# Score rows through DRAM and VectorE's 32x32 transposes in place of TensorE's, in a fused four-layer graph attention kernel

## The chip, the core and the metric

The kernel runs on one core of a Trainium2 chip. Its engines are TensorE (PE, matmuls; its weight loads are listed as PEld), VectorE (DVE), ScalarE (ACT), GpSimd (POOL) and SyncE (SP, which here only issues DMA transfers). Each engine works through its own list of instructions in order and waits at semaphores for the others. The metric is the device time of one execution in microseconds (us).

## The reference: four graph attention layers

There are 128 graphs of 128 nodes, each with 512 float32 features (`x`) and a 128x128 0/1 adjacency matrix (`adj`, int32, symmetric, ones on the diagonal). Four layers follow each other, each of the form `x = x + layer(relu(layernorm(x)), adj)`:

```python
# layer 0: e = leaky_relu(h@W.T@a1 + (h@W.T@a2).T); softmax over columns where adj != 0
x = x + elu(softmax(masked e) @ h)
# layer 1: two attention stages; the first with 4 heads of 256, elu, then one head of 512
xl = (h @ W1).reshape(N, 4, 256); e[s, d, head] = leaky_relu(asrc[s] + adst[d])
h = elu(attention over s, per head, + b1); x = x + attention(h @ W2) + b2
# layer 2: scores from two vectors of 512, the diagonal always allowed
x = x + softmax(masked leaky_relu(src[:, None] + dst[None, :] + b)) @ h
# layer 3: 8 heads of 64
xh = (h @ W_proj) per head; x = x + relu(softmax(masked leaky_relu(a_src[i] + a_dst[j] + b)) @ xh)
```

In every attention a score is a sum of a number that belongs to its row and one that belongs to its column. So a 128x128 tile of scores needs one of the two vectors as a column (one number per partition, which is how the engines produce it) and the other as a row repeated over all 128 partitions.

## The kernel before

The four layers are fused: a graph's `x` tile (128 nodes on partitions, 512 features) is loaded once, goes through all layers in SBUF and is stored. One graph is one generator, `graph(b)`, that yields single instructions. A planner written in the kernel (`Scheduler`) keeps `FLYING = 11` graphs under way and puts their instructions in one order. It estimates when each could start from a table of costs (`Step.estimate`) and gives an engine, among the steps that could start about then, the one with the lowest rank. A rank is the graph's age times the pace of the busiest engine, plus a due time spread over `FLYING` paces, from a rehearsal of one graph. Buffers come from tagged pools of fixed size (`tile_of(tag, bufs, ...)`): a stream that asks for one when none has been returned stands still. As every step is recorded by one line of the planner, nearly all instructions carry line 301 in the profile and are told apart by their tiles' names.

How a column becomes a row over all partitions:

- **By TensorE.** `attended` (layer 0, layer 1's second attention, layer 2) multiplies the column, broadcast to 128x128, with the identity (`T.transpose(pb[:, :P], other.to_broadcast([P, P]), ident)`, line 707): the rows stand in a PSUM bank. In the trace these are `bank<-ident,f` (layers 0 and 2) and `bank<-ident,x` (layer 1).
- **By DRAM.** `rows_in_dram` (608) has VectorE transpose 32x32 squares (`r<-...`, STREAM_TRANSPOSE), then SP writes four short pieces to DRAM (`d<-r`) and a second transfer reads them back, repeated for all partitions. Layer 1's first attention (`e<-d`) and layer 3 work so.
- The last `LATE = 5` graphs use TensorE throughout (`spread`, `add_rows`).

Layer 1's first attention ends with a turn of the four heads' weights: `turned` (588) lets VectorE transpose all 32x32 squares in place, and exchanges the squares by four writes to DRAM and one load (`turned<-e`, `et<-turned`).

Layer 3 (`layer3`, 860) builds its eight heads' scores already turned, which saves that turn. ScalarE first copies the turned mask `m3t` over eight heads into `e` (`e<-m3t`). The row vectors and, later, the negated maxima come through DRAM, and GpSimd adds each to `e` by a DMA that accumulates in SBUF (`added`, 649, `e<-d` on POOL's queue). The maxima need the scores in the other direction too, so SP loads the other vector into `d3` (`d<-d`), and VectorE sums it with the mask `m3` and takes the maxima. Then come eight Prelu, the second accumulating DMA and one Exp over all 1024 columns.

The turned mask comes from TensorE: `graph` (983) transposes `m3` (`bank<-ident,m`), VectorE makes the mask of layer 1 out of it (`m1<-bank,off_diag`), and ScalarE copies it to `m3t`. `load` (967) brings four graphs' `adj` at a time by one transfer (`at`).

Of the kernel before, what the change touches and what calls it, by code (L numbers as in the profile page):

```python
# [21 lines left out]
FLYING = 11  # L22
PATIENCE = .3
LANES = 8
AHEAD = 1
LATE = 5
# [18 lines left out]
class Step:  # L45
# [19 lines left out]
    def estimate(self, name, outs, ins, kw):  # L65

        if name == "dma_start":
            moved = size(outs[0]) * outs[0].shape[0] * 4
            if self.engine == "POOL":
                self.moves = moved / 165e3  # L70
                return 1.0, 3
            run = 4 * min(a.shape[-1] for a in outs + ins)
            self.moves = moved / (280e3 if run > 512 else 220e3)
            busy = 0.5 if max(len(a.shape) for a in outs + ins) > 2 else 0.35
            return busy, (2.2 if moved > 16384 else 0.6)
# [250 lines left out]
def kernel(  # L326
# [62 lines left out]
    off_diag = const.tile([P, P], F32, name="off_diag")  # L389
    nc.vector.tensor_scalar(off_diag, ident, -1.0, 1.0, ALU.mult, ALU.add)  # L390
# [36 lines left out]
    def setup():  # L427
# [7 lines left out]
        for c in range(KC):  # L435
            if c % 2 == 0:
                pair = yield tile_of("e3", 3, H3, P)
                pair = pair.rearrange("p h q -> p (h q)").rearrange("p (c f) -> p c f", c=2)
            w0.append(pair[:, c % 2])
            yield S.dma_start(out=w0[c], in_=l0_w[c * P : (c + 1) * P])  # L440
# [4 lines left out]
        yield Fork(fold_w1())  # L445
        yield from load(1)
# [19 lines left out]
        wa = yield tile_of("e3", 3, H3, P)  # L466
        wa = wa.rearrange("p h q -> p (h q)")[:, : H3 * 2 * K3]
# [120 lines left out]
    def turned(t, squares, tag, bufs):  # L588

        yield V.transpose(squares, squares)
        f = t.shape[1] // R
        d = dram.tile([R, Q, R, f], F32, tag="turned", name="turned")
        yield Group(
            [
                S.dma_start(
                    out=d[:, :, r].rearrange("m b f -> b m f"),
                    in_=t[r * Q : (r + 1) * Q].rearrange("b (m f) -> b m f", m=R),
                )  # L600
                for r in range(R)
            ]
        )
        to = yield tile_of(tag, bufs, R * f)
        yield S.dma_start(out=to, in_=d.rearrange("m b r f -> (m b) (r f)"))
        return to
# [16 lines left out]

    def repeated(cols):
        n = cols.shape[1]
        return cols.unsqueeze(1).to_broadcast([P, Q // n, n])
# [13 lines left out]

    def add_rows(cols, to):

        for g in range(0, cols.shape[1], 4):
            pt = yield from spread(cols[:, g : g + 4])
            part = to[:, g * P : (g + 4) * P]
            yield V.tensor_tensor(part, pt, part, ALU.add)
            give_back(pt)

    def added(to, rows):

        yield G.dma_start(out=to, in_=rows, accum_op=ALU.add)
# [51 lines left out]
    def attended(own, other, mask, values, exact=False):  # L703

        e = yield tile_of("e0", 3, P)
        pb = yield bank()
        yield T.transpose(pb[:, :P], other.to_broadcast([P, P]), ident)
        c, rz = yield from attention(own, [pb[:, :P]], [e], mask, exact)
# [45 lines left out]
    def layer0(xt, mask):  # L754
# [6 lines left out]
        pa, c, rz = yield from attended(f[:, 0:1], f[:, 1:2], mask, h, exact=True)  # L761
# [10 lines left out]
    def layer1(xt, mask, late):  # L772
# [28 lines left out]
        else:  # L801
            to = yield from turned(e, e, "et1", 2)
# [40 lines left out]
        pa, c, rz = yield from attended(gx[:, 1:2], gx[:, 0:1], mask, gx[:, E2:])  # L843
# [4 lines left out]
    def layer2(xt, mask):  # L848
# [6 lines left out]
        pa, c, rz = yield from attended(fb, f[:, 1:2], mask, h)  # L855
# [4 lines left out]
    def layer3(xt, mask, mask_t, late):  # L860

# [8 lines left out]

        e = yield tile_of("e3", 3, H3, P)
        yield A.copy(e, mask_t.unsqueeze(1).to_broadcast([P, H3, P]))
        give_back(mask_t)
# [11 lines left out]
        yield G.tensor_tensor(f, fx[:, :, :E3].rearrange("p h s -> p s h"), b_l3, ALU.add)  # L885
        if late:
            fork = yield Fork(add_rows(f[:, 1], e.rearrange("p h q -> p (h q)")))
        else:
            rows = yield from rows_in_dram(repeated(f.rearrange("p s h -> p (s h)")), 2 * H3)
            d = yield tile_of("d3", 2, H3, P)  # L890
            yield S.dma_start(out=d.rearrange("p h q -> p (h q)"), in_=rows[:, : H3 * P])
            fork = yield Fork(added(e.rearrange("p h q -> p (h q)"), rows[:, H3 * P :]))

        for g in range(0, H3, 4):
            if late:
                d = yield from spread(f[:, 0, g : g + 4])
                part = d.rearrange("p (h q) -> p h q", h=4)
            else:
                part = d[:, g : g + 4]
# [3 lines left out]
                        out=part[:, j],  # L903
                        in0=part[:, j],
                        in1=mask,
# [9 lines left out]
            if late:  # L915
                give_back(d)
        give_back(mask)
        if not late:
            give_back(d)
        yield Join(fork)  # L920
# [3 lines left out]
        fork = None if late else (yield Fork(rows_in_dram(repeated(mx), H3)))  # L924
        for k in range(H3):
            yield A.activation(
                out=e[:, k, :],
                in_=e[:, k, :],
                func=AF.Prelu,
                bias=f[:, 0, k : k + 1],  # L930
                alpha=SLOPE,
            )
        ef = e.rearrange("p h q -> p (h q)")
        fork = yield Fork(add_rows(mx, ef) if late else added(ef, (yield Join(fork))))
        yield Join(fork)
        yield A.activation(out=ef, in_=ef, func=AF.Exp)
        t = yield tile_of("t", 5, D)
        for i in range(2):
# [6 lines left out]
                        lhsT=e[:, k, :],  # L945
# [16 lines left out]
        give_back(e, fx, f)  # L962
        yield V.scalar_tensor_tensor(xt, t, 0.0, xt, ALU.max, ALU.add)
# [3 lines left out]
    def load(b):  # L967
# [3 lines left out]
        if b % AG == 0:  # L971
# [3 lines left out]
            )  # L975
        sched.reached.add(("x", b))

    def not_above_0(a):
        m3 = yield tile_of("m3", 4, P)
        yield V.tensor_scalar(m3, a, 0.0, NEG, ALU.is_le, ALU.mult)  # L980
        return m3

    def graph(b):
        if FLYING + AHEAD <= b + AHEAD < B:
            yield Fork(load(b + AHEAD))
        yield Until(("x", b))
# [3 lines left out]
        yield from layer0(xt, m0)  # L990
        give_back(m0)
        m3 = yield from not_above_0(a)
        m3t = yield tile_of("m3t", FLYING, P)
        m1 = yield tile_of("m1", 8, P)
        pt = yield bank()
        yield T.transpose(pt[:, :P], m3, ident)
        give_back(m3)
        yield V.tensor_tensor(m1, pt[:, :P], off_diag, ALU.mult)
        yield A.copy(m3t, pt[:, :P])
        give_back(pt)  # L1000
        yield from layer1(xt, m1, b >= B - LATE)
# [4 lines left out]
        yield from layer2(xt, m2)  # L1006
        give_back(m2)
        m3 = yield from not_above_0(a)
        yield from layer3(xt, m3, m3t, b >= B - LATE)
        yield S.dma_start(out=out[b], in_=xt)  # L1010

    adjs, xs = {}, {}
    with tc.manual_schedule():
        sched.rehearse(load(0))
        sched.plan(sched.rehearse(graph(0)))
# [59 lines left out]
```

## Time and profile before

| | |
|---|---|
| median of 3 runs | 3332.38 us (3332.28 to 3333.03) |
| the profiled execution's own time | 3333.2 us |
| its span in the profile | 3331.4 us |
| TensorE busy | 3286.5 us, 16252 matmul records |
| weight loads busy | 2577.7 us |
| VectorE busy | 2752.8 us, 11063 instructions |
| ScalarE busy | 2478.1 us |
| GpSimd busy | 1208.4 us, of it 246 DMA issues at 948 ns |
| DMA | 380.90 MB, mean 114 GB/s; SP's queue 248.06 MB, GpSimd's 128.99 MB |

The profile is one execution. "Busy" is the time in which at least one instruction of the engine was under way. The slices cut the span into 40 equal parts, and a digit is the busy share in tenths. In the groups a line reads: source line, engine, operation, output tile from input tiles, shapes, count, then busy time, mean ns of one, and the idle time of the engine just before such instructions with what ended it. A table of stretches gives, for each, the busy time of every engine with its number of instructions, then the clock that TensorE was granted, the DMA engines' busy share and the GB/s they moved. An order of time lists start, duration, engine, operation and count. Program order on an engine is fixed, so an instruction that waits holds up all behind it.

### The profile page before, as it was taken

Reading aid. Unit: us, or ns where it says so; the run is one execution under the profiler, and the core shown is the slowest. Engines: PE = TensorE matmul, PEld = TensorE weight load, DVE = VectorE, ACT = ScalarE, POOL = GpSimd, SP = SyncE. Lnnn points to the kernel's source line nnn. Section 1 sums busy time; section 2 is a strip of 40 time slices with the busy share of each in tenths; the row PEclk is TensorE's granted clock in tenths of the full one; section 3 lists DMA queues with packets and bytes.
Section 4 is the critical chain, followed back from the end, with each engine's and each line's share of the span. In section 5 each row is a group of like instructions: output and inputs, shape, how many; then the busy total and the mean of one; then the engine's idle time right before and its main releaser. Section 6 shows DMA issues by size and latency. Waiting matters only on the chain. (4 is left out here: it accounts for less than half of the span.)

```text
span 3331.4 us, 59808 instructions
## 1 busy us (share of the span) xinstructions
PE 3286.5 (99%) x16252; PEld 2577.7 (77%) x16252; DVE 2752.8 (83%) x11063; ACT 2478.1 (74%) x6932; POOL 1208.4 (36%) x2559
## 2 busy tenths in 40 slices
PE   7999999999999999999999999999999999999997
PEld 5777777777777777777777777777777777777776
DVE  5878888888888888888888888888888888888866
ACT  4677777777777777777777777777777777777764
POOL 1233343343343343333334334334334334334321
PEclk7999999999999999999999999999999999999998
DMA  5144444454445454454545454445445545545430
GB/s 156 50 111 116 118 122 115 121 121 119 113 123 121 116 124 119 114 125 114 120 121 120 116 118 121 121 115 123 118 115 124 121 115 120 121 114 123 93 85 29
DMA packets 253730, 380.90 MB, mean 114 GB/s; under 512 B 59088, under 2 KB 138448, under 8 KB 253392
## 3 DMA queue, kind: packets, MB, share of 16 engines
q1 hardware_dynamic: 213792, 248.06, 25.7%
q0 software_dynamic: 35424, 128.99, 20.8%
q8 instruction: 130, 2.13, 0.3%
q14 instruction: 208, 1.70, 0.2%
q10 hardware_dynamic: 4176, 0.02, 0.1%
HBM read 309.35 MB, written 67.57 MB: 113 GB/s over the span
## 5 line engine op out<-in xcount | busy, mean ns | idle before, releaser
L301 PE MATMUL bank<-w2x,y 128*128 128x257 f32 x4096 | 972.1, 380 | 0.0
L301 PE MATMUL bank<-w1x,ht 128*128 128x344 f32 x3072 | 957.4, 455 | 0.7 <-ACT ht L301 0.7
L301 PEld LDWEIGHTS bank<-w2x,y 128*128 128x128 f32 x4096 | 759.4, 190 | 218.5 <-issue 119.6
L301 PEld LDWEIGHTS bank<-w1x,ht 128*128 128x128 f32 x3072 | 567.7, 191 | 243.3 <-issue 7.8
L301 ACT ACTIVATE h<-xt,st 128x512 f32<-128x512 f32 x512 | 416.5, 814 | 257.4 <-POOL st L301 256.2
L301 POOL TENSOR_SCALAR st<-st 128x1 f32<-128x1 f32 x1024 | 351.4, 347 | 661.8 <-DVE st L301 539.5
L301 ACT ACTIVATE e<-e,c 128x128 f32<-128x128 f32 x1408 | 532.7, 400 | 77.8 <-DVE e L301 59.0
L301 PE MATMUL bank<-wpx,ht 128*128 128x264 f32 x2048 | 501.9, 389 | 1.7 <-ACT ht L301 1.7
L301 PEld LDWEIGHTS bank<-wpx,ht 128*128 128x128 f32 x2048 | 390.5, 191 | 66.5 <-ACT ht L301 2.4
L301 ACT ACTIVATE e<-e,f 128x128 f32<-128x128 f32 x1152 | 386.1, 392 | 2.6 <-POOL st L301 1.5
L301 POOL DMA_DIRECT2D e<-d x246 | 233.3, 948 | 389.1 <-DMA d<-r 208.7
L301 DVE BATCH_NORM_STATS2 st<-xt 128x6 f32<-128x512 f32 x512 | 349.4, 683 | 0.0
L301 PEld LDWEIGHTS bank<-x,e 128*128 128x128 f32 x2048 | 269.4, 193 | 91.4 <-issue 56.7
L301 POOL TENSOR_TENSOR st<-st,minus_half 128x1 f32<-128x1 f32 x512 | 298.5, 585 | 29.4
L301 PE MATMUL bank<-et,xl 128*128 128x128 f32 x2048 | 270.3, 275 | 0.0
L301 PE MATMUL bank<-x,e 128*128 128x65 f32 x2048 | 259.0, 270 | 8.9 <-ACT e L301 8.9
L301 POOL TENSOR_TENSOR f<-f 128x8 f32<-128x8 f32 x128 | 30.7, 240 | 651.3 <-DVE f L301 449.1
L301 PE MATMUL bank<-h,et 128*128 128x512 f32 x512 | 263.8, 597 | 1.8 <-ACT et L301 1.8
L301 PEld LDWEIGHTS bank<-et,xl 128*128 128x128 f32 x2048 | 254.0, 192 | 4.9 <-issue 0.5
L301 DVE TENSOR_TENSOR y<-bank,b 128x512 f32<-128x512 f32 x256 | 176.1, 688 | 97.3 <-PE bank L301 95.8
L301 DVE CUSTOM_DVE_ANT_0 d<-d,m 128x128 f32<-128x128 f32 x984 | 225.3, 284 | 34.9 <-DMA d<-d 33.8
L301 POOL TENSOR_SCALAR m<-m 128x128 f32<-128x128 f32 x128 | 143.3, 1119 | 288.9 <-DVE m L301 266.1
(86 smaller groups left out, 5334.4 us busy)
## 6 DMA issues: line engine op xcount, KB each, us to landing
e<-d POOLq DMA_DIRECT2D x246, 512.0 KB, 7.1
d<-d SPq DMA_DIRECT2D x123, 512.0 KB
xt<-in_x_dram SPq DMA_DIRECT2D x128, 256.0 KB
e<-d SPq DMA_DIRECT2D x128, 256.0 KB
out_dram<-xt SPq DMA_DIRECT2D x128, 256.0 KB
turned<-e SPq DMA_DIRECT2D x492, 64.0 KB
et<-turned SPq DMA_DIRECT2D x123, 256.0 KB
at<-in_adj_dram SPq DMA_DIRECT2D x32, 256.0 KB
```

The costliest lines, as they stand in the source:

```text
L301: method(*args, **kw)
```

## The change

- **Rows.** A new `row(col)` takes TensorE's place in `attended`: VectorE transposes the column's squares, SP writes four pieces of 32 numbers to DRAM (`d<-r`) and reads them back over all partitions (`row<-d`, 64 KB). TensorE's way stays for the last 5 graphs, and in layer 0 for the first `EARLY = 8` graphs.
- **Layer 3** now makes its scores unturned: SP loads the row vectors straight into `e`, VectorE adds the mask and takes the maxima in place, and ScalarE does eight Prelu and eight Exp with a bias by column. Then `exchanged` (once `turned`, now without VectorE's transpose in it) sends the squares through DRAM into `et3`, and VectorE transposes them from there into `e`. The mask copy over eight heads, `d3`, both accumulating DMAs and the second row vector are gone. The last 5 graphs turn their scores by TensorE (`bank<-ident,e`).
- **The turned mask.** `load_turned` loads `adj` a second time, four graphs at once by four transfers, with the 32x32 squares already exchanged (runs of 128 bytes); one VectorE transpose of 128x512 for four graphs turns the squares. `m1` comes from it in one instruction; TensorE's transpose, `m3t` and one `m3` go.
- **The planner.** `FLYING` goes from 11 to 13 (which also sizes the pools of `x`, `adj` and DRAM tiles), small DMAs are costed at 1.3 instead of 0.6 us, runs of at most 128 bytes at a lower rate, and the rehearsed graph is graph 8. `e3` and `w0`'s use of it change shape only; `m3` has 3 buffers instead of 4.

```diff
-FLYING = 11
+FLYING = 13
+EARLY = 8
...
-            self.moves = moved / (280e3 if run > 512 else 220e3)
+            self.moves = moved / (280e3 if run > 512 else 220e3 if run > 128 else 130e3)
...
-            return busy, (2.2 if moved > 16384 else 0.6)
+            return busy, (2.2 if moved > 16384 else 1.3)
...
+        yield Fork(load_turned(0))
         yield from load(1)
...
-    def turned(t, squares, tag, bufs):
-        yield V.transpose(squares, squares)
+    def exchanged(t, tag, bufs):
...
+    def row(col):
+        r = yield tile_of("r", 5, Q)
+        yield V.transpose(r, col.to_broadcast([P, Q]))
+        d = dram.tile([R, Q], F32, tag="d1", name="d")
+        yield S.dma_start(out=d, in_=r[::Q])
+        give_back(r)
+        to = yield tile_of("row", 3, P)
+        yield S.dma_start(out=to, in_=d.rearrange("c b -> (c b)").partition_broadcast(P))
+        return to
...
-    def attended(own, other, mask, values, exact=False):
+    def attended(own, other, mask, values, late, exact=False):
         e = yield tile_of("e0", 3, P)
-        pb = yield bank()
-        yield T.transpose(pb[:, :P], other.to_broadcast([P, P]), ident)
-        c, rz = yield from attention(own, [pb[:, :P]], [e], mask, exact)
+        if late:
+            rows = yield bank()
+            yield T.transpose(rows[:, :P], other.to_broadcast([P, P]), ident)
+        else:
+            rows = yield from row(other)
+        c, rz = yield from attention(own, [rows[:, :P]], [e], mask, exact)
...
-        e = yield tile_of("e3", 3, H3, P)
-        yield A.copy(e, mask_t.unsqueeze(1).to_broadcast([P, H3, P]))
...
+        e = yield tile_of("e3", 3, H3 * P)
         if late:
-            fork = yield Fork(add_rows(f[:, 1], e.rearrange("p h q -> p (h q)")))
+            heads = e.rearrange("p (h c b) -> p h c b", h=H3, b=Q)
         else:
-            rows = yield from rows_in_dram(repeated(f.rearrange("p s h -> p (s h)")), 2 * H3)
-            d = yield tile_of("d3", 2, H3, P)
-            yield S.dma_start(out=d.rearrange("p h q -> p (h q)"), in_=rows[:, : H3 * P])
-            fork = yield Fork(added(e.rearrange("p h q -> p (h q)"), rows[:, H3 * P :]))
+            heads = e.rearrange("p (c h b) -> p h c b", h=H3, b=Q)
+            rows = yield from rows_in_dram(repeated(f[:, 0]), H3, True)
+            yield S.dma_start(out=e, in_=rows)
...
-        fork = None if late else (yield Fork(rows_in_dram(repeated(mx), H3)))
-        for k in range(H3):
-            yield A.activation(
-                out=e[:, k, :],
-                in_=e[:, k, :],
-                func=AF.Prelu,
-                bias=f[:, 0, k : k + 1],
-                alpha=SLOPE,
-            )
-        ef = e.rearrange("p h q -> p (h q)")
-        fork = yield Fork(add_rows(mx, ef) if late else added(ef, (yield Join(fork))))
-        yield Join(fork)
-        yield A.activation(out=ef, in_=ef, func=AF.Exp)
+        for bias, func in ((f[:, 1], dict(func=AF.Prelu, alpha=SLOPE)), (mx, dict(func=AF.Exp))):
+            for k in range(H3):
+                yield A.activation(
+                    out=heads[:, k], in_=heads[:, k], bias=bias[:, k : k + 1], **func
+                )
+        et = []
+        if late:
+            for g in range(0, H3, 4):
+                et += yield from transposed(blocks_of(e)[g : g + 4], "ht", 3)
+        else:
+            to = yield from exchanged(e, "et3", 2)
+            yield V.transpose(
+                e.rearrange("p (h r b) -> p r h b", h=H3, b=Q),
+                to.rearrange("p (r h b) -> p r h b", h=H3, b=Q),
+            )
...
+    def load_turned(b):
+        adjs_t[b // AG] = t = adjp.tile([P, AG, P], I32, tag="at_t", name="at_t")
+        yield Group(
+            [
+                S.dma_start(
+                    out=t[m * Q : (m + 1) * Q].rearrange("b g (r c) -> b (g r) c", r=R),
+                    in_=adj[b : b + AG, :, m * Q : (m + 1) * Q].rearrange(
+                        "g (r b) c -> b (g r) c", r=R
+                    ),
+                )
+                for m in range(R)
+            ]
+        )
...
-        m3 = yield from not_above_0(a)
-        m3t = yield tile_of("m3t", FLYING, P)
-        pt = yield bank()
-        yield T.transpose(pt[:, :P], m3, ident)
-        yield V.tensor_tensor(m1, pt[:, :P], off_diag, ALU.mult)
-        yield A.copy(m3t, pt[:, :P])
+        if b % AG == 0:
+            yield Until(("loaded", b // AG))
+            flat = adjs_t[b // AG].rearrange("p g j -> p (g j)")
+            yield V.transpose(flat, flat)
+            sched.reached.add(("turned", b // AG))
+        yield Until(("turned", b // AG))
+        at = adjs_t[b // AG][:, b % AG, :]
+        m1 = yield tile_of("m1", 8, P)
+        yield V.scalar_tensor_tensor(m1, at, 0.0, neg_off_diag, ALU.is_le, ALU.mult)
```

## The prediction

> **What bounds the kernel now.** I read the busy shares and the 40 slices first, then busy time by stretch, then the order of time on TensorE, then the costliest groups.
>
> ```profile
> PE 3286.5 (99%) x16252; PEld 2577.7 (77%) x16252; DVE 2752.8 (83%) x11063; ACT 2478.1 (74%) x6932; POOL 1208.4 (36%) x2559
> ...
> PE   7999999999999999999999999999999999999997
> ...
> DVE  5878888888888888888888888888888888888866
> ...
> PEclk7999999999999999999999999999999999999998
> ```
>
> TensorE (PE) is full except in the first and last slice. Those are also where its granted clock falls. The stretches:
>
> ```profile
> 30.00:40.00 10.00, 8.23 (x36) 7.03 (x36) 5.57 (x26) 3.45 (x9) 1.48 (x3) 0.50 1.10 290
> ...
> 90.00:100.00 10.00, 8.45 (x47) 6.79 (x46) 9.47 (x26) 8.27 (x24) 1.09 (x3) 1.00 0.09 27
> 100.00:110.00 10.00, 10.00 (x51) 8.14 (x50) 9.47 (x29) 4.50 (x13) 1.21 (x3) 1.00 0.26 79
> ...
> 400.00:2800.00 2400.00, 2400.00 (x11939) 1888.22 (x11938) 2025.89 (x8213) 1837.97 (x5161) 916.54 (x1907) 1.00 0.49 119
> ```
>
> The columns are PE, weight load, VectorE (DVE), ScalarE (ACT), GpSimd (POOL), clock, DMA share, GB/s. From 400 to 2800 us PE is busy 2400.00 of 2400 us at full clock. A usual graph has 125 matmul records (32 with w2x, 24 with w1x, 16 each with wpx, et and x, 6 of attention, 15 transposes), so 11939 records are 95.5 graphs and the pace is 25.1 us a graph. In it DVE is busy 2025.89 / 95.5 = 21.2 us and ACT 19.2 us.
>
> Busy is not the same as full, since matmul records overlap. The starts decide:
>
> ```profile
> 1610.14 1.00 PE L301 MATMUL bank<-x,e 128*128 128x65 f32 x8
> 1610.98 0.28 PE L301 MATMUL bank<-ident,m 128*128 128x128 f32 x1
> 1611.09 0.27 PE L301 MATMUL bank<-ident,e 128*128 128x128 f32 x1
> 1611.20 1.90 PE L301 MATMUL bank<-w2x,y 128*128 128x257 f32 x8
> 1612.93 0.39 PE L301 MATMUL bank<-wpx,ht 128*128 128x264 f32 x1
> ```
>
> A transpose lasts 0.27 us, but the next matmul starts 0.11 us after it. Eight matmuls with w2x take 1612.93 - 1611.20 = 1.73 us, 0.216 each. Over the 2400 us the mean distance from one start to the next is that of its kind's median (ident,f 109 ns, ident,m 116, w2x 217, w1x 289), so no gap is left and each matmul taken away saves its distance. The Trainium skill (Perfetto Trace Analysis, Identifying the Most-Contended Engine) says matmul busy time is a poor measure of how near TensorE is to its limit, and that weight-load busy time is a better one. That row is 77%, so by the rule a quarter of PE might be free, removed transposes might be worth nothing, and the sum would stay at 3333. The start distances decide against that here.
>
> ```profile
> L301 PE MATMUL bank<-ident,f 128*128 128x128 f32 x376 | 86.3, 275 | 4.8 <-POOL f L301 2.8 <-DVE f L301 2.0
> ...
> L301 DVE STREAM_TRANSPOSE e<-e 128x512 f32<-128x512 f32 x123 | 85.3, 693 | 2.0 <-ACT e L301 1.8
> ...
> L301 DVE STREAM_TRANSPOSE r<-f 128x32 f32<-128x32 f32 x246 | 50.8, 207 | 34.8 <-POOL f L301 26.4
> ```
>
> The first is one of the three kinds of PE transpose that go; the others price what comes. Then who waited for whom (total, times, longest), on the engines and in SP's own DMA queue, for layer 3's score rows as they are today:
>
> ```profile
> DVE d L301 <- DMA d<-d: 33.8, 44, 2.0
> ```
>
> ```profile
> SPq L301 <- DMA d<-r: 508.9, 339, 5.1
> ```
>
> **The change part by part, TensorE.** Counted in the two programs: transposes of score columns (ident,f) fall from 376 to 58, of x from 128 to 5, of the mask (ident,m) from 128 to 0; transposes of e rise from 404 to 444 (the last five graphs' layer 3 now turns its scores at the end). Net 318 + 123 + 128 - 40 = 529 fewer, by 0.11 us: **-58.2 us**. Nothing else on PE changes. A usual graph goes from 25.1 to 24.7 us.
>
> **VectorE**, per graph. Added: three column transposes of 128x32 (3 x 0.207 = 0.62), one layer 3 transpose of 128x1024 (twice the 0.693 row, 1.39), a quarter of adj's 128x512 (0.17). Gone: one 128x32 (0.21), one of two not_above_0 masks (0.22). The mask m1, the score sums and their maxima change operands, not count; the row for 128x128 sums is 284 ns from SBUF and 287 from PSUM. Net +1.75, so 23.0 of 24.7 us: 93%, where it had 84%. The large transpose writes in strides that no row shows. Bounds: 1.39 (a row of half its size, and the 128x32 rows read in strides without cost) and double that, 2.77, which would make 24.4 of 24.7. I take 1.39, the row of the same operation. Either way it lies beside PE.
>
> **ScalarE**, per graph: gone are the copy of the mask over eight heads (1.03), m3t (0.27) and the Exp over 1024 (1.05); added are eight Exp of 128. One such takes 0.39 in its row, but the last graph's chain of eight takes 2.35 us in the trace, 0.29 each. Net 0, at most +0.8 by the 0.39: 81% of 24.7. Hidden.
>
> **GpSimd** loses 246 adding transfers at 0.948 us of issue, 233 us in all, and the 7.1 us each took to land.
>
> **SP and DMA.** SP issues more: per usual graph 3 row writes, 3 row loads, one for adj_t (four per four graphs), and in layer 3 five exchange transfers, with four writes fewer there and the score load kept. Eight more at 0.34 to 0.45 us are some 3 us, on about 8. Behind a row write its load waits at SP (508.9 / 339 = 1.5 us a time), and other graphs' loads and the output are queued behind that: three such waits more a graph and one more for layer 3's exchange, 6 us. 8 + 3 + 6 and today's waits of 508.9 / 123 = 4 stay under 24.7, with less to spare than now. In bytes the 129 MB of adding transfers are traded for 129 MB of exchange at a DMA share of 0.49, so bandwidth is free in the middle. Of small transfers the change adds 722 (361 of 0.5 KB and 361 of 64 KB). The skill (DMA: Bandwidth & Descriptors, Rules for kernel authors) speaks against such transfers: under 64 KB one pays mostly overhead, and its section on one DMA's anatomy gives about 2 us of fixed cost each. By that page a row's two hops would be an estimated 4 us late, 12 us more in a graph's life, and the sum would not move as long as other graphs cover it; no run here shows a row of this kind yet.
>
> **Latency.** A row through DRAM costs two hops at about 1.5 us plus issue, transpose and queue; I call it 5, thrice 15 us a graph. In layer 3 two landings of 7.1 go, and an exchange comes (write to read about 6 us in the same trace for layer 1, then the landing): +10. Net some +11 us in a graph's life, against 13 x 24.7 - 11 x 25.1 = 45 us more that 13 graphs in flight allow. Cover: the other twelve graphs.
>
> **Ramp and tail.** In the first 40 us DMA runs at a share of 0.88 to 1.10 and the clock at half, so new traffic there delays PE: four second adj loads of 256 KB, one more first load and two more x are 1.75 MB, at 290 GB/s 6 us if all comes before the weights, 0 if none does. I take 4. First graphs keep their layer 0 rows on PE; the x transposes begin only at 113 us. In the tail the last layer 3 trades an addition (0.70) and a 1.05 Exp for eight short ones (2.35) and a transpose with copy: +1. More graphs in flight may fill the tail better or put off its last graph: -10 to +10.
>
> **Sum** against the profiled execution (3333.2, span 3331.4): 3333.2 - 58.2 + 4 + 1 = 3280.0. It lies 0.8 above the median of 3332.38, so 3279 for a median.
>
> **Rivals.** (1) *PE keeps its pace only nearly.* The cushion of ready work in front of PE shrinks as DVE goes to 93%. At 95% DVE, 90 to 100 us shows PE at 8.45 and 100 to 110 at 10.00, so both happen. PE at 99% instead of 100% for the middle 3100 us costs 31: 3310; from 0.4% to 1.5%: 3291 to 3326.
> (2) *VectorE becomes the bound because its queue waits for landings.* Each of the three row sums and the layer 3 transpose stands in DVE's order, and everything behind it waits when its DMA is late. DVE has 24.7 - 23.0 = 1.7 us a graph free: waits over 0.43 us each make it the bound, over 0.53 each end above today's pace. At 0.77 (33.8 / 44, what a late score load costs today when it waits) it is 26.1 a graph, +1.0 over today for 123 graphs: 3455. At 0.6: 25.4, 3370. Against it: today's same wait falls on 44 of 123 loads, 0.27 us as a mean, below 0.43.
> (3) *The transposes were free*, so that the 0.11 us stays as a gap: 3333 to 3338. Against it: the start distances.
>
> **How the numbers follow.** PE stays full: 0.62 (own range 3265 to 3291: ramp 0 to 6, tail -10 to +10). Rival 1: 0.17. Rival 2: 0.13. Rival 3 or gain and losses cancelling: 0.05. Below 3265, a ramp or tail that shrinks: 0.03. Executions agree within 0.03%; 0.2% (7 us) is about what can be told from no change: faster 0.82, same 0.05, slower 0.13. The range 3260 to 3332 leaves out rival 2 (0.13), the cancelling case's upper half and the gains below 3260, some 0.17.
>
> **What would show it.** Right: PE 100% from 400 to 2800 us with about 97 graphs there, ident,f x58, no ident,m, DVE 90 to 94% and no large idle before the sums on row. Wrong: idle before e<-row put down to DMA d or row, PE nines with idle released by DVE or ACT, the layer 3 transpose well over 1.39 us, or a lower clock after 200 us.

## The result and the profile after

The changed kernel takes 3290.93 us (median of 4 runs, 3290.09 to 3293.56) against 3332.33 us before (4 runs, 3330.88 to 3333.03). The ratio is 0.9881, 95% interval 0.9869 to 0.9894. The forecast was 3279, range 3260 to 3332: the direction and the range held, the value was 12 us too low. The profiled execution after took 3290.5 us, with a span of 3288.7.

The busy shares of the page after, and TensorE's, VectorE's and the clock's row of the 40 slices:

```profile
PE 3233.0 (98%) x15723; PEld 2529.1 (77%) x15723; DVE 2839.9 (86%) x11308; ACT 2546.5 (77%) x7582; POOL 911.3 (28%) x2313
...
PE   6999999999999999999999999999999999999997
...
DVE  6778888988888988888898988898888888888875
...
PEclk6999999999999999999999999999999999999998
```

529 matmul records are gone (16252 to 15723), and TensorE is full but for the ends, as before. The stretches after (PE, weight load, VectorE, ScalarE, GpSimd, clock, DMA share, GB/s):

```profile
30.00:40.00 10.00, 8.80 (x35) 7.23 (x35) 4.63 (x18) 3.67 (x9) 0.00 (x0) 0.50 1.11 312
40.00:50.00 10.00, 0.48 (x3) 0.39 (x2) 9.59 (x28) 0.22 (x2) 0.00 (x0) 0.50 0.91 163
50.00:60.00 10.00, 3.47 (x5) 1.05 (x5) 8.19 (x27) 4.62 (x10) 3.13 (x9) 0.50 0.00 0
60.00:70.00 10.00, 5.05 (x7) 1.64 (x7) 8.70 (x30) 3.50 (x8) 0.78 (x2) 0.50 0.00 1
...
400.00:2800.00 2400.00, 2399.02 (x11720) 1882.38 (x11719) 2137.87 (x8550) 1913.93 (x5713) 688.29 (x1741) 1.00 0.46 131
```

and the stretch of before beside the second of them:

```profile
40.00:50.00 10.00, 10.00 (x32) 6.42 (x33) 7.12 (x22) 4.71 (x11) 0.00 (x0) 0.79 0.16 55
```

The middle is nearly as forecast (PE busy 2399.02 of 2400 us). The start is not: between 40 and 70 us TensorE works 9 of 30 us, at half clock. The groups after that answer to those shown of before, and the two new ones:

```profile
L302 DVE CUSTOM_DVE_ANT_0 e<-row,m 128x128 f32<-128x128 f32 x361 | 101.7, 282 | 51.3 <-DMA row<-d 50.7
...
L302 DVE STREAM_TRANSPOSE e<-et 128x1024 f32<-128x1024 f32 x123 | 148.6, 1208 | 0.2 <-issue 0.2
...
L302 DVE STREAM_TRANSPOSE e<-e 128x512 f32<-128x512 f32 x123 | 86.6, 704 | 4.9 <-ACT e L302 4.9
```

```profile
L302 PE MATMUL bank<-ident,f 128*128 128x128 f32 x58 | 11.3, 288 | 5.0 <-DVE f L302 4.8 <-POOL f L302 0.2
```

The waits after, of VectorE for the new rows and of SP's queue for the row writes:

```profile
DVE e L302 <- DMA row<-d: 50.7, 60, 3.0
```

```profile
SPq L302 <- DMA d<-r: 393.1, 450, 4.5
```

**A yardstick for all runs.** In the middle of the kernel before no gap is left between matmuls. So I give every matmul record the mean distance to the next start that its kind has there (400 to 2800 us), and call the sum of these over a whole run its *work*: the time TensorE needs if it never waits and its clock is full. Kinds that do not occur there (112 records of the setup, and 80 of the last graphs after the change) count by their shape, or at 0.11 us. The span less the work is the *loss*, so it holds waits, late starts and slow clock together.

| us | before | after | difference |
|---|---|---|---|
| span | 3331.4 | 3288.7 | -42.7 |
| work | 3250.1 | 3191.5 | -58.6 |
| loss, first 400 us | 44.9 | 59.5 | +14.6 |
| loss, 400 us to 200 before the end | 0.6 | 9.0 | +8.4 |
| loss, last 200 us | 35.8 | 28.8 | -7.0 |

The work fell by what was forecast (58.2), and the middle stays within 9.0 us of it. What was missed lies in the loss, +14.6 of it at the start.

### The profile page after: what moved, and what is told of

Same layout as the page of the kernel before. It is cut to its first block, busy times and chain, and to the rows that moved or that the text cites. A ratio compares the mean times of both kernels' runs of the same rounds, so it can differ in the third digit from the quotient of the medians.

```text
span 3288.7 us, 60292 instructions
## 1 busy us (share of the span) xinstructions
PE 3233.0 (98%) x15723; PEld 2529.1 (77%) x15723; DVE 2839.9 (86%) x11308; ACT 2546.5 (77%) x7582; POOL 911.3 (28%) x2313
## 4 chain that ended last, share of the span: by engine, by line
PE 95%; DVE 2%; DMA 2%; ACT 1%; SPq 0%; issue 0%; POOL 0%; ACTq 0%; DVEq 0%; POOLq 0%
PE bank L302 95%; DVE e L302 0%; SPq L302 0%; ACT e L302 0%; DMA d<-r 0%; DVE products L302 0%; DVE t L302 0%; POOL st L302 0%; DMA row<-d 0%; DMA w1x<-in_L_gnn_W_dram 0%; ACT h L302 0%; DMA xt<-in_x_dram 0%; DVE xt L302 0%; DVE st L302 0%; DMA at<-in_adj_dram 0%
## 5 line engine op out<-in xcount | busy, mean ns | idle before, releaser
L302 PE MATMUL bank<-w2x,y 128*128 128x257 f32 x4096 | 959.1, 381 | 0.0
L302 ACT ACTIVATE e<-e,f 128x128 f32<-128x128 f32 x2176 | 739.4, 392 | 18.2 <-DVE c L302 18.0
L302 ACT ACTIVATE e<-e,c 128x128 f32<-128x128 f32 x1408 | 543.5, 396 | 78.7 <-DVE c L302 59.7
L302 DVE CUSTOM_DVE_ANT_0 e<-e,m 128x128 f32<-128x128 f32 x1496 | 344.0, 284 | 4.2 <-DMA e<-d 3.0
L302 POOL TENSOR_TENSOR st<-st,minus_half 128x1 f32<-128x1 f32 x512 | 313.2, 612 | 40.6 <-POOL st L302 0.2
L302 ACT COPY xl<-bank 128x344 f32<-128x344 f32 x384 | 169.5, 442 | 188.9 <-PE bank L302 187.6
L302 PEld LDWEIGHTS bank<-x,e 128*128 128x128 f32 x1968 | 248.5, 192 | 19.7 <-issue 8.6
L302 POOL TENSOR_SCALAR m<-m 128x128 f32<-128x128 f32 x128 | 86.3, 674 | 619.3 <-DVE m L302 503.8
L302 DVE SCALAR_TENSOR_TENSOR xt<-bank,c,xt 128x512 f32<-128x512 f32 x256 | 192.0, 750 | 75.5 <-PE bank L302 70.3
L302 PE MATMUL bank<-x,e 128*128 128x65 f32 x1968 | 246.7, 268 | 0.0
```

What stands on the lines that cost most here:

```text
L302: method(*args, **kw)
```

## The experiments

All are edits of the changed kernel unless said otherwise. In the table "rows" are the score rows of layers 0, 1 (second attention) and 2, "mask" the turned mask (TensorE's transpose, or adj's second load), "n" the graphs in flight; loss is given for the three stretches of the table above. The ratio is to runs of the kernel before that belong to the same set (medians 3331.51 for e1 to e4, 3330.69 for e5 to e8, 3331.05 for e9 to e12). Work and loss come from one profiled execution each, which need not be the median one: it lies 4.8 us under the median for e4, 3.1 under it for e3, 2.5 under it for e1, and 5.1, 4.2 and 2.9 over it for e10, e7 and e11. So a difference of some us between losses is not yet a difference between kernels.

| kernel | rows | layer 3 | mask | n | median us | ratio (95%) | work | loss: start, middle, end |
|---|---|---|---|---|---|---|---|---|
| before | TensorE | old | TensorE | 11 | 3332.33 | 1 | 3250.1 | 44.9, 0.6, 35.8 |
| after | DRAM | new | 2nd load | 13 | 3290.93 | 0.9881 (0.9869 to 0.9894) | 3191.5 | 59.5, 9.0, 28.8 |
| e1 | DRAM | new | 2nd load, early | 13 | 3289.70 | 0.9874 (0.9858 to 0.9891) | 3191.5 | 55.6, 9.1, 29.1 |
| e2 | DRAM | new | 2nd load | 11 | 3359.09 | 1.0080 (1.0065 to 1.0095) | 3191.5 | 77.9, 46.3, 41.6 |
| e3 | TensorE | new | 2nd load | 13 | 3484.83 | 1.0457 (1.0441 to 1.0472) | 3230.9 | 67.5, 158.0, 23.5 |
| e4 | DRAM | new | TensorE | 13 | 3301.66 | 0.9906 (0.9891 to 0.9921) | 3206.4 | 47.2, 14.8, 26.7 |
| e5 | TensorE | old | TensorE | 13 | 3342.23 | 1.0033 (1.0021 to 1.0045) | 3250.1 | 51.7, 10.7, 28.0 |
| e6 | TensorE | new | 2nd load | 11 | 3377.20 | 1.0139 (1.0122 to 1.0156) | 3230.9 | 58.2, 58.7, 28.5 |
| e7 | DRAM | old | 2nd load | 13 | 3428.69 | 1.0293 (1.0274 to 1.0313) | 3195.8 | 72.7, 127.0, 35.5 |
| e8 | DRAM | new | as e1, one fold on GpSimd | 13 | 3291.18 | 0.9882 (0.9867 to 0.9897) | 3191.5 | 58.0, 9.4, 28.5 |
| e9 | DRAM, all | new | 2nd load | 13 | 3291.10 | 0.9879 (0.9864 to 0.9894) | 3190.6 | 56.2, 14.8, 28.5 |
| e10 | TensorE | old | 2nd load | 13 | 3370.38 | 1.0118 (1.0103 to 1.0133) | 3235.2 | 57.5, 51.5, 29.3 |
| e11 | TensorE | new | TensorE | 11 | 3321.54 | 0.9970 (0.9958 to 0.9981) | 3245.8 | 43.5, 5.3, 28.1 |
| e12 | DRAM | new | as e1, other order | 13 | 3288.41 | 0.9872 (0.9857 to 0.9886) | 3191.5 | 58.4, 11.4, 25.3 |

### The start: where the 15 us went

The order of time of the changed kernel, from SP's issue of adj's second loads to the first matmuls of layer 1 (start, duration; idle time before in brackets):

```profile
38.01 10.82 SPq L302 DMA_DIRECT2D at_t<-in_adj_dram  x16
...
49.51 0.28 DVE L302 TENSOR_SCALAR e<-e,f 128x128 f32<-128x128 f32 x1
...
50.70 0.48 PE L302 MATMUL bank<-ident,e 128*128 128x128 f32 x1 [10.22 <-ACT e L302]
...
67.09 0.70 DVE L302 STREAM_TRANSPOSE at_t<-at_t 128x512 int32<-128x512 int32 x1
67.83 0.29 DVE L302 SCALAR_TENSOR_TENSOR m<-at_t,neg_off_diag 128x128 f32<-128x128 int32 x1
...
73.67 1.93 PE L302 MATMUL bank<-w1x,ht 128*128 128x344 f32 x3
```

Graph 0's second load is a stream of its own beside the one that loads everything else, and the planner puts it last: all 16 transfers of the four second loads go out from 38 us on, behind the weights and all x. In the program the layer 1 of every graph comes behind that mask, so the first matmul of layer 1 starts at 73.67 us; before it was this one:

```profile
43.49 2.82 PE L301 MATMUL bank<-w1x,ht 128*128 128x344 f32 x8
```

In between TensorE has only layer 0, and that waits for VectorE, which has taken up the sums that fold weights into `w2x` (41.56 to 49.5 us, eleven in a row). Between 50 and 70 us the DMA engines move next to nothing (share 0.00 in the stretches above), and VectorE is never seen waiting for `at_t`: the turn comes at 67.09 us because of its place in VectorE's order, behind these sums and the layer 0 of the other first graphs. That the planner placed it there because it expected the load late is likely, and not shown.

**e1_early_turned**

```diff
         yield Fork(fold_w1())
-        yield Fork(load_turned(0))
+        yield from load_turned(0)
```

> The changed kernel with one line different: the first turned load of adj (graphs 0 to 3) is issued where it stands in the setup, after the w1x loads, instead of as a fork that comes after all other first loads. Theory A (the missing 16 us went to the start: SP issues the turned adj last, at 38 us, layer 1's mask of graph 0 is late, and the sixteen w2x sums on VectorE stand in front): first matmul with w1x at 42 to 50 us instead of 73.7, TensorE's loss up to 400 us falls from 59.5 to 44 to 50 us, time 3276 to 3283. Theory B (the start is slow because 13 graphs and the second adj bring 1.75 MB more into a full DMA): the order of loads does not help, 3288 to 3296.

Measured 3289.70 us, in theory B's range. The order that theory A names is what held layer 1 up, as far as that goes: layer 1 now begins at 39.81 us, and the loss from 40 to 80 us falls from 30.6 to 14.9. But from 80 to 200 us it rises from 5.4 to 18.4. The stretches of e1 there:

```profile
80.00:90.00 10.00, 1.11 (x4) 0.71 (x4) 9.72 (x36) 5.44 (x20) 1.61 (x3) 0.50 0.19 52
90.00:100.00 10.00, 9.65 (x34) 7.53 (x35) 8.31 (x22) 8.00 (x29) 3.31 (x9) 0.69 0.16 39
```

```profile
83.93 1.11 PE L302 MATMUL bank<-ident,h 128*128 128x128 f32 x4 [7.11 <-ACT h L302]
90.35 3.78 PE L302 MATMUL bank<-et,xl 128*128 128x128 f32 x16 [5.30 <-DMA et<-exchanged]
```

TensorE stands again, first for the normalised input `h`, then for layer 1's exchanged weights, VectorE is 97% busy (with layer 3's weight fold among other things), and the clock falls to half. DMA is busy 0.19 and 0.16 there, so theory B's reason, a full DMA, is not what stands here either. Moved 40 us on, the stall costs nearly as much.

**e8_early_turned_pool_fold**: e1's edit, and

```diff
-                yield V.tensor_tensor(
+                yield G.tensor_tensor(
                     p3, w[:, :, E3:], pairs[:, :, s * K3 : (s + 1) * K3], ALU.mult
```

> The first run's edit (graph 0's second adj load ahead of the next loads) together with the eight products of layer 3's weight fold on GpSimd instead of VectorE. Alone the first edit took 15.7 us of loss out of 40 to 80 us and gave 13 back between 80 and 200 us, where VectorE was 97% busy with those folds. Theory A: VectorE's queue of folds is what TensorE waits for there; eight products of 0.69 us less free 5.5 us of it: 3280 to 3286. Theory B: the folds only move, GpSimd's products are slower than VectorE's and graph 0's layer 3 waits for them: 3288 to 3298.

Measured 3291.18: theory B's range. The loss from 80 to 200 us is 22.3. Taking the eight products off VectorE in this way does not help. They take 1.31 us each on GpSimd against 0.68 on VectorE, so the run does not separate VectorE's load from folds that come later.

**e12_early_turned_x3_patience**: e1's edit, and

```diff
-PATIENCE = .3
+PATIENCE = .1
...
-        fx = yield tile_of("x3", 3, H3, E3 + K3 + 1)
+        fx = yield tile_of("x3", 4, H3, E3 + K3 + 1)
```

> The first run's edit with one more buffer for layer 3's projected features (x3: 4 in place of 3) and the planner's patience for VectorE and ScalarE at 0.1 in place of 0.3 us. Nothing of the work changes (3191.5). Theory A: the loss in the middle (8) and after the start (18 between 80 and 200 us) is a matter of the order in which VectorE and ScalarE take ready steps and of streams that stand for x3: 3276 to 3285. Theory B: it is the folds and the masks that VectorE must do before graph 0 comes through, in whatever order: 3286 to 3294.

Measured 3288.41, theory B, with a start loss of 58.4. Its interval and those of e1 and of the changed kernel overlap: none of the three is shown to be faster than another.

**e9_early0**

```diff
-EARLY = 8
+EARLY = 0
```

> The changed kernel with layer 0's score rows of the first eight graphs through DRAM as well (EARLY = 0), so that all usual graphs are alike. TensorE's work is 0.9 us less (8 transposes). Theory A: in the first 60 us SP's queue and the DMA engines are full of weight loads (DMA share 0.9 and over), so the rows of the first graphs come late, and TensorE has nothing else yet: loss up to 200 us grows by 15 to 40: 3304 to 3332. Theory B: TensorE waits there for graph 0's mask and VectorE's folds anyway (loss of 30.6 between 40 and 80 us), and the rows come in time beside that: 3287 to 3294.

Measured 3291.10, theory B: keeping layer 0's rows of the first eight graphs on TensorE is worth nothing that can be measured. Theory B's reason, that they wait for the same things, was not tested further.

**e4_mask_by_pe**

```diff
-        if b % AG == 0:
-            yield Until(("loaded", b // AG))
-            flat = adjs_t[b // AG].rearrange("p g j -> p (g j)")
-            yield V.transpose(flat, flat)
-            sched.reached.add(("turned", b // AG))
-        yield Until(("turned", b // AG))
-        at = adjs_t[b // AG][:, b % AG, :]
+        m3 = yield from not_above_0(a, "m3", 3)
         m1 = yield tile_of("m1", 8, P)
-        yield V.scalar_tensor_tensor(m1, at, 0.0, neg_off_diag, ALU.is_le, ALU.mult)
+        pt = yield bank()
+        yield T.transpose(pt[:, :P], m3, ident)
+        give_back(m3)
+        yield V.tensor_tensor(m1, pt[:, :P], off_diag, ALU.mult)
+        give_back(pt)
```

(`load_turned` and its calls go too.)

> The changed kernel with layer 1's mask turned by TensorE again and no second load of adj: 128 transposes at 0.116 us, +14.9 us of TensorE work. Theory A: the start recovers its 10 to 14 us (loss up to 400 us 45 to 50), so the time stays at 3288 to 3297 in spite of the added work. Theory B or a loss elsewhere: 3302 to 3309.

Measured 3301.66, just under theory B's range; the start's loss lies in theory A's. Without the second load the start loses 47.2 instead of 59.5 us, and the work is 14.9 us higher. So the second load puts 12.3 us of loss into the start, most of the 14.6 that the change lost there; the other 2.3 come with the rest. The size is from one execution each, and e4's is 4.8 us under its median. As a whole the second load is still worth 10.7 us by the medians (3301.66 to 3290.93). VectorE's wait for rows in e4:

```profile
DVE e L302 <- DMA row<-d: 7.0, 12, 2.1
```

In the changed kernel it is 50.7 us, so most of that wait goes with the second load.

### Thirteen graphs in flight

**e2_flying11** (the changed kernel) and **e5_before_flying13** (the kernel before):

```diff
-FLYING = 13
+FLYING = 11
```

> The changed kernel with 11 graphs in flight instead of 13. Theory A: the start stays slow (loss up to 400 us 55 to 62), and the middle shows whether the two more graphs were needed for the rows' latency: if they were, TensorE's loss between 400 us and the last 600 us grows from 8 to 20 or more and the time is 3300 to 3330; if not, 3285 to 3295. Theory B: fewer first loads, the start recovers some 5 us, 3280 to 3287.

```diff
-FLYING = 11
+FLYING = 13
```

> The kernel before with 13 instead of 11 graphs in flight and nothing else changed (3332 us before; TensorE's work, the matmul records by the start distances of their kinds, stays 3250.1). Theory A: the old kernel's 11 graphs already covered its latencies, as its 0.2 us of loss between 400 and 2731 us says; 13 change only ramp and tail, by -5 to +10: 3327 to 3342, so that the 68 us which two graphs are worth in the changed kernel belong to the latencies that the change adds. Theory B: a part of the gain is the number of graphs alone (fuller ramp and tail, by the 7 us that the changed kernel's tail gained): 3310 to 3326.

The changed kernel with 11 takes 3359.09 us, 68 more than with 13, above every range named, and 0.8% more than before the change. Its loss rises by 18.4 us at the start, 37.3 in the middle and 12.8 at the end. Between 400 and 2800 us TensorE has one kind of wait, for the layers' normalised input `h`, and it comes back every 100.5 us (901.29, 1001.77, 1102.24), that is every four graphs. As idle time it is 12.1 us; the rest of the loss are late starts and what comes after 2800 us. That wait, and VectorE's for rows in the whole run:

```profile
PE bank L302 <- ACT h L302: 12.1, 23, 0.5
```

```profile
DVE e L302 <- DMA row<-d: 8.6, 8, 2.2
```

The old kernel with 13 takes 3342.23 us: 0.3% slower than with 11, 0.2 us past theory A's upper end. So the two extra graphs give nothing by themselves; the changed kernel needs them. That they cover the latency of its rows, as theory A has it, is not shown: with 11 VectorE waits for rows 8.6 us, with 13 it is 50.7. The rhythm of four graphs is that of adj's second load, and e6 below, with 11 graphs and its rows on TensorE, loses more in the middle. Rows through DRAM with 11 graphs and without the second load were not run.

e5 also tells where two small terms of the result belong. Its middle loses 10.7 us with the old instructions and VectorE at 81%:

```profile
400.00:2800.00 2400.00, 2400.00 (x11886) 1882.19 (x11885) 1944.09 (x8191) 1875.41 (x5135) 874.18 (x1904) 1.00 0.49 119
```

In it one matmul with `w1x` and one with `w2x` a graph start 55 ns late (95 times each, 10.4 us together), although PE reads 2400.00 of 2400 busy. The changed kernel has the same 55 ns at two matmuls with `w1x` and two with `w2x` in every four graphs, 5.2 of its 9.0 us, beside a few short waits for `et`. So most of the 9.0 us is of a kind that needs no new load on VectorE. It is not a matter of 13 graphs alone: e11 below has such late starts at 95 matmuls with `et`, with 11 graphs. What causes them stays open.

### One part at a time: they do not add up

**e3_rows_by_pe**, in `attended`:

```diff
-        if late:
+        if True:
             rows = yield bank()
             yield T.transpose(rows[:, :P], other.to_broadcast([P, P]), ident)
```

> The changed kernel with all rows in attended by TensorE again (layers 0 and 2 and layer 1's second attention); layer 3, the turned adj and 13 graphs as in the change. 361 transposes come back at 0.109 us: +39.4 us of TensorE work. Theory A (TensorE is the bound, a transpose costs its start distance): 3326 to 3334. Rival (rows through DRAM cost the middle its 8 us of stalls, and these go again): 3317 to 3325. If the transposes were free: 3285 to 3293.

Measured 3484.83, 150 us over either theory. The work rose by the 39.4 us of the transposes; the middle's loss rose by 149. The order of time of e3 shows one of its stalls, which comes back every 105.81 us, that is every four graphs:

```profile
1016.12 1.00 PE L302 MATMUL bank<-x,e 128*128 128x65 f32 x8
...
1017.18 0.70 DVE L302 STREAM_TRANSPOSE at_t<-at_t 128x512 int32<-128x512 int32 x1
...
1019.06 0.68 DVE L302 CUSTOM_DVE_ANT_0 products<-h,u 128x512 f32<-128x512 f32 x1
...
1019.80 0.32 PE L302 MATMUL bank<-ident,f 128*128 128x128 f32 x1 [2.68 <-DVE f L302]
...
1020.78 1.12 PE L302 MATMUL bank<-ident,h 128*128 128x128 f32 x4 [0.65 <-ACT h L302]
```

In this kernel a row transpose on TensorE costs more than its 0.11 us: it is a place in TensorE's order where everything behind it waits until VectorE has come to the sum that gives the column. VectorE is only 81% busy in e3's middle, yet at 1016 to 1020 us its queue has no gap. With the row through DRAM that wait lies on VectorE and SP, and TensorE's order has one rendezvous (a place where it must wait for another engine) less. The rendezvous alone does not make the loss: the kernel before and e11 have the same row transposes and lose 0.6 and 5.3 us in the middle.

**e6_rows_by_pe_11**: e3 with `FLYING = 11`.

> The changed kernel with all row transposes left on TensorE and 11 in place of 13 graphs in flight. Work 3231. The run with rows on TensorE and 13 graphs lost 249 us, 158 of them between 400 us and the tail. Theory A: those stalls come from the planner's due times at 13 graphs, and at 11 the order is as good as in the kernel before (loss 81 to 100): 3312 to 3335. Theory B: they come from what TensorE's own row transposes wait for in the new layer 3 and mask (VectorE's queue), whatever the number of graphs, and fewer graphs cover less: 3470 to 3560.

Measured 3377.20, between the two theories: fewer graphs help here (middle loss 58.7 against 158.0), and don't mend it. Its stalls also come back every four graphs, but 10 and 36 us after the turn of `at_t`, so the turn's 0.70 us is not directly before them.

**e11_layer3_only_11**: e6 with e4's mask, that is, the kernel before with layer 3 new, and with the planner's new figures (costs of small DMAs, rehearsed graph).

> The kernel before with the new layer 3 alone: score rows of the other layers and the mask by TensorE, 11 graphs in flight. Work 3245.7. Theory A: in the run with all rows by TensorE at 11 graphs the middle lost 50 us in a pattern that repeats every four graphs, and what comes every four graphs is the turn of adj's second load; without it the order is as good as before: loss 81 to 95: 3327 to 3342. Theory B: the new layer 3 (its exchange and turn make a graph's life 10 us longer) needs more than 11 graphs wherever rows stand in TensorE's order: loss 130 to 160: 3376 to 3406.

Measured 3321.54, a little under theory A: the middle loses 5.3. e6 and e11 differ in the mask alone: with 11 graphs and the rows in TensorE's order, the second load costs 53 us of loss in the middle. With 13 graphs and the rows through DRAM (after against e4) it costs none there. With 11 graphs and the rows through DRAM (e2) the middle loses 46.3, close to e6's 58.7. So with 11 graphs both kernels with the second load lose about alike, whichever way their rows go, and e2's need of 13 may come from that load. e11 also shows that the new layer 3, whose exchange and turn I had charged with 10 us of latency, needs no further graphs: by itself, at 11, it is 9.5 us faster than before, 4.3 of it work (the last five graphs' transposes).

**e7_old_layer3**: layer 3 as before, and

```diff
         m3 = yield from not_above_0(a, "m3", 3)
-        yield from layer3(xt, m3, late)
+        m3t = yield from not_above_0(at, "m3t", 3)
+        yield from layer3(xt, m3, m3t, late)
```

> The changed kernel with layer 3 as it was before: the mask copied over eight heads, two accumulating transfers by GpSimd, the second row vector, one Exp; its turned mask is made by VectorE from adj's second load (0.22 us a graph). Work 3196 (+4.4 by the last five graphs). VectorE has 1 us a graph less than in the changed kernel. Theory A: the 9 us that TensorE lost between 400 us and the tail come from VectorE's load (89% busy), so they go, and latency is covered: 3280 to 3288. Theory B: layer 3's form is neutral for TensorE or its accumulating transfers (7 us each) need more cover: 3290 to 3310.

**e10_mask_only_13**: the kernel before with that mask and 13 graphs; rows by TensorE.

> The kernel before with adj's second load in place of TensorE's mask transpose, and 13 graphs in flight; all score rows and layer 3 as before. Work 3236.0 (128 transposes less). The run with the old layer 3 and rows through DRAM lost 127 us between 400 us and its last 200. Theory A: that loss came from row landings held up beside the accumulating transfers (VectorE waited 171 us for row, against 51 in the changed kernel), so without such rows it is gone; what remains is the loss of the old kernel at 13 graphs (90) and the start (8 to 12): 3330 to 3342. Theory B: it came from the mask made by VectorE or the order: 3390 to 3440.

e7 took 3428.69, far over both theories, e10 3370.38, between its two. e7's waits:

```profile
DVE e L302 <- DMA row<-d: 171.1, 97, 5.8
...
DVE d L302 <- DMA d<-d: 96.2, 79, 4.5
...
DVE e L302 <- DMA e<-d: 48.7, 38, 3.5
```

and in e10:

```profile
DVE d L301 <- DMA d<-d: 107.7, 105, 3.2
```

This looks like rival 2's mechanism, in another kernel: 171.1 / 361 = 0.47 us a row, and 316 us of VectorE's waits for DMA in the three lines, 2.6 a graph, where the changed kernel has 0.14 a row. With the accumulating transfers still there, one lands 8.2 us after its issue (7.1 before, 6.0 in e5, by the page's list of DMA issues), and DMA is busy 0.54 of the middle (0.46 in the changed kernel). e7 and e10 differ in the rows and in the planner's figures (small DMAs at 1.3 or 0.6 us, rehearsed graph 8 or 0), and e7 loses 75 us more in the middle. What is shown is that with rows and second load in place the new layer 3 is worth 138 us (e7 against after). That it is the accumulating transfers in the old one that delay the rows is a likely reading of these waits; a run that changed their traffic alone was not made. The second load has a part in such waits as well: e5 and e10 differ in the mask alone, and VectorE's wait for `d<-d` goes from 49.4 to 107.7 us.

What stays open is why the second load of adj costs so much in e10, e6, e3 and, it seems, e2. They lose in patterns of four graphs (e10 less evenly), which is the rhythm of that load; but its turn is not what stands before the stalls in e6, and the load also changes the order that the planner writes (its due times come from a graph that has the turn in it, three of four graphs have not).

## Why the prediction was right, and where it was not

- **TensorE is the bound, and each transpose is worth its start distance.** Right: 529 x 0.11 = 58.2 forecast, 58.6 by the yardstick. That yardstick uses the same distances, so the two agree by their making; the test is that the changed kernel's middle takes only 9.0 of 2690 us more than its work. The Trainium skill (Perfetto Trace Analysis, Identifying the Most-Contended Engine) would have weight-load busy time, beside the share of peak arithmetic, judge TensorE's headroom: it reads 77% before and after, and the time did fall with the transposes, so here the start distances are the better measure. In e3 the 361 row transposes of this work, put back, cost far more than their distances, so the price held for the change as a whole and not for each part.
- **VectorE.** Forecast 93% of the middle, and 90 to 94% as a sign of being right; measured 89% (2137.87 of 2400), just below. The 128x1024 transpose in strides takes 1.21 us; 1.39 was taken. "Busy" also moves with the order alone: with all its instructions unchanged, e5 has 2661.3 us against 2752.8 before.
- **ScalarE.** 80% (1913.93 of 2400). The forecast's net 0 is 19.2 of 24.7 us, 78%; its 81% is the sum with the +0.8 that it gave as the most.
- **SP and landings.** The write of a row holds up SP for 393.1 / 450 = 0.87 us a time (1.5 before). VectorE waits 50.7 us for rows, 0.41 a graph; rival 2 needed 1.7. The Trainium skill's fixed cost of about 2 us a transfer (DMA: Bandwidth & Descriptors, Anatomy of one DMA) is given in that section for transfers that GpSimd issues, and these are SP's. The waits here neither confirm nor contradict it: a wait shows only what is not covered.
- **Latency.** With 13 graphs the middle lost 9.0 us, so the cover held, and e2 shows that 13 were needed: two graphs less, and the gain becomes a loss. What they cover is not shown to be the latency that the forecast added up: e2's waits for rows are short (8.6 us) and its stalls come with the rhythm of the second load, which the forecast did not count here. The 10 us that it charged to layer 3's exchange need no cover beyond 11 (e11).
- **Ramp: the step that failed.** It was priced in bytes, "1.75 MB, at 290 GB/s 6 us if all comes before the weights, 0 if none does. I take 4". Measured up to 400 us: 14.6. Bytes were not the cost: from 50 to 70 us DMA moves next to nothing and TensorE still stands. The second load stands last in SP's order, and its turn stands behind weight folds and layer 0 in VectorE's, so layer 1 of the first graph begins 30 us later. The two ends bounded the bytes only, and with 12.3 us (e4) the load lies outside them. Issuing the load earlier (e1, e8, e12) moved the loss more than it removed it. The forecast's "clock at half" for the first 40 us is also too wide: the profile before has 1.00 in the first 20 us and 0.51 and 0.50 in the next two stretches of 10.
- **Tail.** +1 taken (-10 to +10), measured -7.0. e5 and e11 gain the same with only one part each (28.0 and 28.1 against 35.8), so the parts do not add up and the cause is open. That the tail came out 8.0 better than taken, just as the middle lost 8.4 that were not in the sum, is luck.
- **Rival 1** gave 0.4% to 1.5% of the middle lost; 9.0 us of 2690 is 0.33%. The loss exists, just below that. The cause given for it is not needed: e5 loses 10.7 us with VectorE at 81%.
- **The sum**: -58.6 + 14.6 + 8.4 - 7.0 = -42.6 against -53 forecast.

One assumption was not examined, and it does not hold: the forecast added up the parts as if they were independent. That the whole came out near their sum is in part luck. Of the kernels that leave a part out, only e4 and e11 beat the kernel before; e2, e3, e6, e7 and e10 lose 0.8% to 4.6%, though each has less work than before.

## What to carry to other kernels

When one engine has no gap between starts, price a removed instruction by its start distance; but look also at what it waits for, since an instruction in the bound engine's order is a rendezvous too, and in some orders (e3) that costs more than its time. Moving work to DMA may pay only together with other changes, here a new layer 3 and two more graphs: change these together, and try each alone to know which carries the gain. A term priced as independent is a guess until a run leaves out its partner. For a ramp, follow the first item through all the queues in order, the issuing one and that of the engine that must finish it, instead of counting bytes.

## What was not expected of the hardware

**After a wait of under 3 us TensorE's clock can be halved.** In e3 TensorE waits 2.68 us (above). The stretches after it:

```profile
1020.00:1023.00 3.00, 2.35 (x8) 1.75 (x8) 2.97 (x10) 2.38 (x6) 0.21 (x1) 0.53 0.00 0
...
1026.00:1030.00 4.00, 4.00 (x17) 2.95 (x17) 3.85 (x16) 3.91 (x14) 0.00 (x0) 1.00 0.45 114
```

The trace's clock records give half speed for 3413 ns from 1020.16 us on, and the four transposes there take 1.12 us, where the changed kernel's take 0.60 in its middle. So each round loses 5.8 us to 3.7 us of waiting. The Trainium skill (TensorE: Matmul & The Clock Gate, HAM oscillation) tells to avoid idle gaps over about 3.4 us; here 2.96 us from the start of one matmul to the next was enough. The length alone does not decide: in e10 waits of 1.99 us (ending at 2820.68) and 2.04 us (3006.23) come with such a half-speed stretch, one of 2.36 us (2079.30) does not. Half-speed stretches of e3 follow each other at 105.81 us, which is 31 times 3413 ns; that the stall and the clock's window keep step is what the records show, why they do was not tried.

**The large transpose is not dearer in strides.** 128x1024 read and written in strides takes 1.21 us, the 128x512 in place 0.70: 1.7 times for twice the data.

**"PE 2400.00 of 2400" does not say that no time is lost.** In e5 10 us are missing there by start distances.
